# A four-value GpSimd operation behind the gathers of each tap of a deformable convolution

## The chip, the core and the metric

The kernel runs on one core of a Trainium2 chip. The core has five engines that run side by side, each with a queue of its own and in the order of that queue: TensorE (PE in the profile, its weight loads PEld) multiplies matrices, VectorE (DVE) and ScalarE (ACT) work elementwise, GpSimd (POOL) here issues indirect DMAs, and SyncE (SP) issues plain DMAs. Sixteen DMA engines, shared by all queues, move the data. The metric is the time of one execution on the device in microseconds (us), as the median of several runs.

## What is computed

The input is a picture batch of 4 x 256 channels x 64 x 64. Three deformable 3x3 convolutions follow a normalisation over the channels; then the result is added to the input and each of the 16,384 pixels goes as a token through a top-2-of-8 expert network. Of the reference, cut to the part that the change touches:

```python
K = 9
def _bilinear(feat, ys, xs):              # feat [B,C,H,W], ys and xs [B,K,H,W]
    y0, x0 = jnp.floor(ys), jnp.floor(xs)
    wy, wx = (ys - y0)[:, None], (xs - x0)[:, None]
    y0i, x0i = y0.astype(jnp.int32), x0.astype(jnp.int32)
    v00, v01 = _gather(feat, y0i, x0i), _gather(feat, y0i, x0i + 1)
    v10, v11 = _gather(feat, y0i + 1, x0i), _gather(feat, y0i + 1, x0i + 1)
    return v00*(1-wy)*(1-wx) + v01*(1-wy)*wx + v10*wy*(1-wx) + v11*wy*wx

def _deform_layer(x, w_off, b_off, w, b, dilation=1):
    om = conv3x3(x, w_off) + b_off        # 27 channels: 18 offsets, 9 masks
    ...
    sampled = _bilinear(x, ys, xs) * mask[:, None]
    return jnp.einsum('bikhw,oik->bohw', sampled, wk) + b[None, :, None, None]

for wo, bo, w, b in params:               # three layers
    x = jax.nn.relu(_deform_layer(x, wo, bo, w, b, dilation=1))
...
t = t + _L0_ffn_ref(_ln_t(t), ...)        # softmax gate, top 2 of 8 experts, gelu
```

For every pixel and every one of the nine taps, four neighbours are read at a place that the data decide, weighted, and multiplied by the tap's 256 x 256 weights.

## The kernel before

All arithmetic is in float32. There are twelve stages, one for each layer and picture; `run` (L1037) lists their order. A stage has eight blocks (NB) of 512 pixels, four tiles of 128 pixels each (TPB). `main_block` (L482) runs one block: nine taps (K), and for each tap two calls of `samples` (L494) with two tiles each. So a tap has four gathers, a block 36, and the whole program 12 x 8 x 36 = 3456, in 864 taps.

One gather (L503) is an indirect DMA on the POOL queue: for each of 128 pixels it fetches one row of 1024 floats, the four neighbours with 256 channels each, from a table in DRAM into a tile `g`. That is 512 KB. DVE then combines the neighbours in two steps (L509 into `g`, L514 into a tile `s`), ACT scales `s` (L517), TensorE transposes it (L532, in `turn`), ACT copies the transposed pairs to `sT` (L535), and `finish` multiplies them by the tap's weights into `acc` (L555). The pool of `g` tiles has GB = 10 buffers, two and a half taps: the eleventh gather waits until L514 has read the first. The pool of `s` tiles has eight. `turn` runs LAG = 2 pairs behind `samples`.

Work of other parts is woven in between the taps. `step` (L1001) advances the offset convolutions, the tables of the next layer and the gate; `pump` (L992) advances three lanes of the expert network. Of these, `fetch` (L790) puts three indirect DMAs on the POOL queue for each expert tile (weights `w` at L800, two token tiles `zt` at L812), and `combine_fetch` (L905) puts two (`gy`, L915) for each token tile. A helper `after` (L1007) pins an instruction behind a given one in the order that the framework works out; `self.gathered` is the newest gather, `self.last` the newest L514. So POOL's queue holds the gathers in order, and `w`, `zt` and `gy` between them behind the fourth gather of a tap. Apart from a few constants at the start, POOL has no arithmetic.

Of the kernel before, what the change touches and what calls it, by code (L numbers as in the profile page):

```python
# [8 lines left out]
F32 = mybir.dt.float32  # L9
I32 = mybir.dt.int32  # L10
AF = mybir.ActivationFunctionType
ALU = mybir.AluOpType
AX = mybir.AxisListType

P = 128
# [102 lines left out]
class Weave:  # L118
# [40 lines left out]
    def constants(self):  # L159
        nc, cst, ins = self.nc, self.cst, self.ins  # L160
        self.ident = cst.tile([P, P], F32, name="ident")
        make_identity(nc, self.ident)

        self.strips = cst.tile([P, Q], F32, name="strips")
        nc.vector.tensor_tensor(
            self.strips, self.ident[:, 0:Q], self.ident[:, Q : 2 * Q], ALU.add
        )
        for g in range(2, NQ):
            nc.vector.tensor_tensor(
                self.strips, self.strips, self.ident[:, g * Q : (g + 1) * Q], ALU.add  # L170
            )
        self.base = cst.tile([P, NB, TPB, K, 2], F32, name="base")
        nc.sync.dma_start(self.base.rearrange("p n t k d -> p (n t k d)"), ins["base"])
        self.wo, self.bo, self.bk = [], [], []
        for l in range(NL):
            queue = nc.sync if l == 0 else nc.gpsimd
            wo = cst.tile([P, K, CC, Q], F32, name=f"wo_{l}")
            queue.dma_start(wo, ins[f"conv_w_off{l}"].rearrange("k (c p) o -> p k c o", p=P))
            bo = cst.tile([P, 1], F32, name=f"bo_{l}")
            queue.dma_start(bo, ins[f"conv_b_off{l}"].rearrange("(o a) -> o a", a=1))  # L180
            bk = cst.tile([P, CC], F32, name=f"bk_{l}")
            queue.dma_start(bk, ins[f"conv_b{l}"].rearrange("(c p) -> p c", p=P))
            self.wo.append(wo)
            self.bo.append(bo)
            self.bk.append(bk)
        self.wk = [None] * K

    def room(self, tag, shape, name, gat=True):

        if not (self.starting and gat):  # L190
            return self.big.tile([P, *shape], F32, tag=tag, name=name)
        g = self.gat.tile([P, 2, 2, C], F32, tag="g", name=name)
        return g.rearrange("p x s f -> p (x s f)").rearrange("p (a b) -> p a b", a=shape[0])
# [288 lines left out]
    def main_block(self, i, n, wins):  # L482
        l, b = self.stages[i]
        plan = self.plans.pop((l, b, n))
        for k in range(K):
            for t0 in range(0, TPB, 2):
                ss = self.samples(i, n, k, t0, plan)
                self.pairs.append((i, n, k, t0, wins, ss))
                if len(self.pairs) > LAG:
                    self.turn()  # L490
            self.step(k)
            self.pump()

# [642 lines left out]
```

## Time and profile before

| | us |
|---|---|
| median of 10 runs | 6802.03 |
| lowest and highest | 6792.87, 6808.45 |
| the profiled execution's own time | 6816.85 |
| its span, first to last instruction | 6815.1 |

The profile is one execution. Its page gives the busy time of each engine, the same in 40 slices of 170 us, the chain of work that ended last, and the groups of instructions by source line. Further views of the same trace used below are tables of busy time by stretch (a busy time and, in brackets, a count for each engine, then the granted TensorE clock, the busy share of the DMA engines and GB/s), lists of waits (who waited for whom, us in total, times, the longest), and lines in order of time (start, duration, engine, line, operation, and in brackets the idle time before it and what ended it). A POOL duration of a DMA is the time in which GpSimd makes it, not the time in which the data move. The twelve stages start at 95, 614, 1054, 1502, 1961, 2459, 2977, 3508, 4055, 4569, 5083 and 5782 us of the span; the last gather is made at 6382, and behind it the last expert tiles are finished.

### The profile page before, as it was taken

The page shows a single profiled execution, that of the slowest core. Times are in us where ns is not written, and L with a number is a line of the kernel's source. Part 1 is how long each engine was busy: PE and PEld are TensorE (multiplying, and loading weights), DVE is VectorE, ACT ScalarE, POOL GpSimd, SP SyncE. Part 2 cuts the span into 40 slices and gives each one's busy share as a digit, 9 for nine tenths or more (in the row PEclk, how much of TensorE's full clock was granted, in tenths as well). Part 3 has the DMA queues.
Part 4 walks back from the last instruction along what each step waited for, and adds up shares of the span by engine and source line. Part 5 has one row for each costly group of instructions (what it writes and reads, how often), then busy time and mean ns, then how long its engine had stood idle before and what let it go on. Part 6 is the DMA issues. An engine that isn't in the chain of part 4 may idle for free.

```text
span 6815.1 us, 88985 instructions
## 1 busy us (share of the span) xinstructions
PE 6222.2 (91%) x26500; PEld 3526.9 (52%) x26500; DVE 4960.5 (73%) x11467; ACT 3280.5 (48%) x7141; POOL 4450.6 (65%) x4245
## 2 busy tenths in 40 slices
PE   7998888889999999999999999999998899988887
PEld 3443344444445555555555555555555566655665
DVE  6887778779999666668888777667878555688521
ACT  3554555555555445445554454445554444454322
POOL 4664766666667666666667777666666666677643
PEclk8999999999999999999999999999999999999998
DMA  8998999999999999899998999989998887899744
GB/s 283 355 352 301 365 350 374 356 350 389 379 394 353 326 353 335 323 332 354 352 360 310 361 360 369 325 328 341 346 344 301 294 291 272 290 350 331 243 136 125
DMA packets 800319, 2223.73 MB, mean 326 GB/s; under 512 B 104728, under 2 KB 302872, under 8 KB 794080
## 3 DMA queue, kind: packets, MB, share of 16 engines
q0 software_dynamic: 551200, 1947.35, 77.4%
q1 hardware_dynamic: 248640, 270.69, 11.7%
q8 instruction: 215, 3.52, 0.2%
q14 instruction: 264, 2.16, 0.1%
HBM read 2160.68 MB, written 196.40 MB: 346 GB/s over the span
## 4 chain that ended last, share of the span: by engine, by line
PE 71%; ACT 8%; DMA 7%; DVE 7%; issue 4%; POOL 3%; SPq 0%; ACTq 0%; DVEq 0%; POOLq 0%
PE acc L555 36%; PE tp L532 10%; PE ph L856 7%; PE po L357 7%; PE py L874 7%; DMA g<-tab,idx 5%; ACT sT L535 3%; DVE g L509 2%; ACT s L517 2%; DVE s L514 2%; POOL gy L915 1%; PE pm L371 1%; POOL g L503 1%; POOL zt L812 1%; PE tpv L325 1%
## 5 line engine op out<-in xcount | busy, mean ns | idle before, releaser
L503 POOL DMA_INDIRECT g<-tab,idx x3456 | 3652.7, 1057 | 1802.5 <-DVE s L514 659.4
L555 PE MATMUL acc<-sT,wk 128*128 128x512 f32 x6912 | 3389.3, 604 | 151.7 <-ACT sT L535 136.9
L509 DVE SCALAR_TENSOR_TENSOR g<-g,cf 128x512 f32<-128x512 f32 x3456 | 2559.0, 742 | 400.8 <-DMA g<-tab,idx 397.1
L514 DVE SCALAR_TENSOR_TENSOR s<-g,cf 128x256 f32<-128x256 f32 x3456 | 1660.4, 482 | 756.1 <-PE tp L532 474.1
L535 ACT COPY sT<-tp 128x512 f32<-128x512 f32 x1728 | 1001.3, 586 | 1836.7 <-PE tp L532 1831.9
L517 ACT ACTIVATE s<-s,cf 128x256 f32<-128x256 f32 x3456 | 1641.5, 508 | 447.1 <-DVE s L514 408.1
L555 PEld LDWEIGHTS acc<-sT,wk 128*128 128x128 f32 x6912 | 1162.6, 192 | 967.4 <-issue 655.9
L532 PEld LDWEIGHTS tp<-ident,s 128*128 128x128 f32 x6912 | 883.0, 143 | 1354.7 <-issue 654.8
L532 PE MATMUL tp<-ident,s 128*128 128x128 f32 x6912 | 1254.1, 281 | 190.9 <-ACT s L517 174.8
L856 PE MATMUL ph<-fzT,w 128*128 128x256 f32 x2608 | 687.6, 396 | 60.1 <-ACT fzT L844 33.6
L874 PE MATMUL py<-w,hT 128*128 128x256 f32 x2608 | 653.2, 389 | 31.8 <-ACT hT L866 26.7
L856 PEld LDWEIGHTS ph<-fzT,w 128*128 128x128 f32 x2608 | 483.9, 196 | 189.3 <-ACT fzT L844 61.5
L874 PEld LDWEIGHTS py<-w,hT 128*128 128x128 f32 x2608 | 475.3, 192 | 164.1 <-ACT hT L866 68.2
L866 ACT ACTIVATE hT<-ph,w 128x256 f32<-128x256 f32 x652 | 282.1, 471 | 450.3 <-PE ph L856 431.6
L812 POOL DMA_INDIRECT zt<-z,tok x326 | 334.6, 1026 | 161.7 <-issue 88.3
L357 PE MATMUL po<-win,wo 128*32 128x504 f32 (+1 forms) x2304 | 357.4, 598 | 5.0 <-ACT win L301 2.6
L800 POOL DMA_INDIRECT w<-in_W,wrow x163 | 178.1, 1092 | 266.4 <-issue 102.6
L915 POOL DMA_INDIRECT gy<-ys,slots x256 | 261.5, 1021 | 111.7 <-issue 65.2
L892 DVE TENSOR_TENSOR y<-py,w 128x512 f32<-128x512 f32 x163 | 111.5, 684 | 218.1 <-PE py L874 218.0
L930 DVE SCALAR_TENSOR_TENSOR ta<-gy,cw,ta 128x256 f32<-128x256 f32 x256 | 120.4, 480 | 137.3 <-DMA gy<-ys,slots 78.1
L357 PE MATMUL po<-win_pre,wo 128*32 128x504 f32 (+1 forms) x1152 | 187.0, 627 | 2.0 <-ACT om L366 2.0
L357 PEld LDWEIGHTS po<-win,wo 128*32 128x32 f32 x2304 | 73.1, 110 | 177.9 <-issue 142.7
(154 smaller groups left out, 2927.8 us busy)
## 6 DMA issues: line engine op xcount, KB each, us to landing
tab<-hv SPq DMA_DIRECT2D x512, 128.0 KB
g<-tab,idx POOLq DMA_INDIRECT x3456
ys<-y SPq DMA_DIRECT2D x163, 256.0 KB
tab<-h_pre SPq DMA_DIRECT2D x128, 256.0 KB
wk<-in_conv_w SPq DMA_DIRECT2D x99, 256.0 KB
xc_pre<-in_x SPq DMA_DIRECT2D x32, 512.0 KB
xr_tok<-in_x SPq DMA_DIRECT2D x32, 512.0 KB
t<-t_tok SPq DMA_DIRECT2D x32, 512.0 KB
```

Of the source, the lines that this page charges most:

```text
L357: nc.tensor.matmul(po[g * Q : (g + 1) * Q, :].rearrange("q (r w) -> q r w", w=W)[:, :, x0:x1], lhsT=self.wo[l][:, 3 * ky + kx, c, :], rhs= ...
L503: self.gathered = nc.gpsimd.indirect_dma_start(out=g.rearrange("p x s f -> p (x s f)"), out_offset=None, in_=self.table(*self.stages[i]), ...
L509: nc.vector.scalar_tensor_tensor(g[:, :, 0, :], g[:, :, 1, :], cf[:, j, 0:1], g[:, :, 0, :], ALU.mult, ALU.add,)
L514: self.last = nc.vector.scalar_tensor_tensor(s, g[:, 1, 0, :], cf[:, j, 1:2], g[:, 0, 0, :], ALU.mult, ALU.add)
L517: nc.scalar.activation(s, s, AF.Copy, scale=cf[:, j, 2:3])
L532: self.turned = nc.tensor.transpose(tp[:, c, u * P : (u + 1) * P], ss[u][:, c * P : (c + 1) * P], self.ident)
L535: nc.scalar.copy(self.sT[:, :, t0 * P : (t0 + 2) * P], tp)
L555: nc.tensor.matmul(acc[:, o, :], lhsT=self.wk[k][:, c, o * P : (o + 1) * P], rhs=sT[:, c, :], start=(k == 0 and c == 0), stop=(k == K - 1 ...
L812: self.nc.gpsimd.indirect_dma_start(out=zt, out_offset=None, in_=grp.zd, in_offset=bass.IndirectOffsetOnAxis(ap=grp.tok[:, j : j + 1], axi ...
L856: nc.tensor.matmul(ph[:, h, :], lhsT=w1[:, o : o + P], rhs=zT[:, c, :], start=(c == 0), stop=(c == CC - 1),)
L874: nc.tensor.matmul(py[:, u, :], lhsT=hT[h // 2][:, h % 2, u * P : (u + 1) * P], rhs=w2[:, h * C : (h + 1) * C], start=(h == 0), stop=(h == ...
L915: self.nc.gpsimd.indirect_dma_start(out=g, out_offset=None, in_=self.ys[grp.i % 3], in_offset=bass.IndirectOffsetOnAxis(ap=grp.slots[:, i, ...
```

## The change

A tile `rest` of 128 partitions x 4 floats is set to one at the start. Behind the four gathers of each tap, GpSimd raises it to the power of itself, in place; the value stays one and nothing reads it. `self.after(self.gathered)` pins the operation behind the tap's fourth gather.

```diff
@@ constants
         self.wk = [None] * K
+        self.rest = cst.tile([P, 4], F32, name="rest")
+        nc.gpsimd.memset(self.rest, 1.0)
@@ main_block
                 self.pairs.append((i, n, k, t0, wins, ss))
                 if len(self.pairs) > LAG:
                     self.turn()
+            with self.after(self.gathered):
+                self.nc.gpsimd.tensor_tensor(self.rest, self.rest, self.rest, ALU.pow)
             self.step(k)
             self.pump()
```

In the built program POOL's 4250 instructions keep their order, and 865 are added: the memset and 864 operations on `rest`, each ahead of the `w`, `zt` and `gy` fetches that stand behind the same gather. Each of the 864 waits for POOL's own semaphore, that is for the operation on `rest` of the tap before. The other engines issue the same instructions; their order differs in 102 of 17,802 places on PE, 56 of 11,469 on DVE, 58 of 7143 on ACT and 3 of 1166 on SP, where neighbours change places.

## The prediction

> **What bounds the kernel now.** First the page, for who is busy over the whole span and what a gather costs:
>
> ```profile
> span 6815.1 us, 88985 instructions
> PE 6222.2 (91%) x26500; PEld 3526.9 (52%) x26500; DVE 4960.5 (73%) x11467; ACT 3280.5 (48%) x7141; POOL 4450.6 (65%) x4245
> PEclk8999999999999999999999999999999999999998
> L503 POOL DMA_INDIRECT g<-tab,idx x3456 | 3652.7, 1057 | 1802.5 <-DVE s L514 659.4
> ```
>
> POOL seems to have a third of its time free. It has not: there is an idle stretch of about 0.30 us before each gather even where nothing is waited for, as the lines of POOL in order of time show, first from a stage without spare, then from one with it:
>
> ```profile
> 3812.93 0.94 POOL L503 DMA_INDIRECT g<-tab,idx  x1 [0.30 <-issue]
> 3814.18 0.95 POOL L503 DMA_INDIRECT g<-tab,idx  x1 [0.30 <-issue]
> 3817.94 1.19 POOL L800 DMA_INDIRECT w<-in_W,wrow  x1 [0.30 <-ACT s L517]
> 3819.44 1.02 POOL L812 DMA_INDIRECT zt<-z,tok  x1 [0.30 <-issue]
> ...
> 2511.58 0.97 POOL L503 DMA_INDIRECT g<-tab,idx  x1 [0.30 <-issue]
> 2512.86 0.94 POOL L503 DMA_INDIRECT g<-tab,idx  x1 [0.30 <-issue]
> 2519.37 1.21 POOL L503 DMA_INDIRECT g<-tab,idx  x1 [5.57 <-DVE s L514]
> ```
>
> So POOL is charged with its busy time and 0.305 us (the median idle time before an indirect DMA in the trace) for each instruction. Over the span: 4450.6 + 4201 x 0.305 = 5732 us of 6815, 84%. By stretch, from the table of busy times:
>
> ```profile
> 1502.00:1961.00 459.00, 418.38 (x1773) 218.04 (x1774) 421.99 (x1101) 246.01 (x543) 311.94 (x288) 0.97 1.01 387
> 2459.00:2977.00 518.00, 491.08 (x2092) 276.36 (x2091) 355.44 (x701) 257.72 (x575) 337.12 (x330) 1.00 0.91 333
> 3655.00:4121.00 466.00, 429.88 (x1853) 233.89 (x1852) 355.27 (x759) 225.84 (x495) 361.78 (x343) 0.99 0.97 355
> 6018.00:6212.00 194.00, 161.28 (x608) 87.04 (x608) 175.04 (x460) 90.87 (x188) 152.12 (x137) 0.95 0.97 359
> ```
>
> The last bracketed pair of a row is POOL's. Stage 3 (1502 to 1961): 311.9 + 288 x 0.305 = 400 of 459, 59 us spare on 72 taps, 0.8 us a tap; there DVE (92%) and the DMA engines bound. Stage 5 (2459 to 2977): 438 of 518, 80 us spare, 1.1 us a tap; TensorE bounds at 95%. But 3655 to 4121, where `w`, `zt` and `gy` fetches stand between the gathers: 361.8 + 343 x 0.305 = 466.4 of 466. POOL is full. So it is from 6018 to 6212: 193.9 of 194. These are 63 and 27 taps. The waits of DVE say what that means for the rest of the core; the first row is from 3655 to 4121, the second from 2459 to 2977:
>
> ```profile
> DVE g L509 <- DMA g<-tab,idx: 76.4, 66, 6.0
> ...
> DVE g L509 <- DMA g<-tab,idx: 2.8, 5, 0.8
> ```
>
> In stage 5 DVE hardly ever waits for a gather. From the semaphore updates of the landings, gathers there lie ready for a median of 7.7 us before L509 takes them; from 3855 to 4055 it is 0.03 to 0.13 us. So a later gather is covered in most stages and is late at once where POOL is full.
>
> **The change part by part.** Removed: nothing. Moved: two neighbours change places in under 1% of the positions on PE, DVE, ACT and SP; no row of these is longer for it, and I cost it at 0, hidden by the same cover of several us; without that cover a swap is worth at most one L509, 0.74 us, some fifty times, 37 us either way. The memset stands among the table fills before 95 us, where POOL then idles 57 us for the first table: 0. The wait for POOL's own semaphore is for the operation of the tap before, over 5 us old: 0. No DMA and no other queue gets an instruction.
>
> Added: 864 operations on four values. Queued behind each on POOL are the next gather, or `w`, `zt` and `gy`; DVE waits for the gathers, TensorE for `zt` and `w`. The trace has no power and no arithmetic between gathers, so its price X is bounded. Below by POOL's small operations at the start:
>
> ```profile
> 37.35 0.31 POOL L247 TENSOR_SCALAR_AFFINE_SELECT upper<-ones 128x128 f32<-128x128 f32 x1
> 37.60 0.15 POOL L259 IOTA part_i<- 128x1 int32 x1
> 37.69 0.26 POOL L264 IOTA row_i<- 128x128 int32 x1
> ```
>
> IOTA on one value takes 0.15 us and starts before its neighbour has ended, the next one 0.09 us later. Above by the longest thing that POOL does again and again, a gather, 1.06 us. A power is nearer to the arithmetic rows than to a gather, but above the simplest: I take X = 0.4, about the geometric mean of 0.15 and 1.06. To this comes the idle time: one more of 0.305 at most; at least none, and if the 0.30 us runs on while the operation is at work, up to 0.305 of X is hidden. I take 0.1. So the delay d for each tap is 0.5 us, with 0 (0.15 hidden in the gap) and 1.36 (1.06 + 0.305) as ends.
>
> Then I walked the POOL rows of the trace in order: d is added behind every fourth gather; each idle time is used up for what it has over 0.305; a lag that exceeds the time for which that gather would lie ready is added to the end and shifts all that follows. That charges DVE's lateness in full. Result, in us added to the end, by stage 0 to 11, for d = 0.5: 2, 6, 2, 2, 9, 3, 0, 29, 10, 4, 18, 30, sum 115. The check by hand: the two full stretches are 90 taps x 0.5 = 45 us; the remaining 70 come from shorter full stretches in stages 4 and 8 to 11, and from each stage's first gathers. For other delays: d = 0.1 gives 20, 0.2 gives 42, 0.4 gives 90, 0.7 gives 170, 1.0 gives 305, 1.36 gives 548. Above 0.7 it bends upwards because it passes the spare of 0.8 to 1.1 us of the other stages.
>
> The profiled execution's own time is 6816.85, 1.75 over its span and 0.2% over the median of 6802.03. The walk is a difference, so it goes on the median: 6802 + 115 = 6917.
>
> [...]
>
> **Rivals.**
> (A) The operation is as long as a gather. d is 1.0 to 1.36, POOL has no spare in nearly any stage and becomes the bound of the whole: 7107 to 7350. For it: no row shows a power, and AFFINE_SELECT and IOTA do far simpler things. Against: four values for each partition, next to 128 in 0.31 us.
> (B) It is hidden. It fits into the 0.30 us that POOL idles before each gather, d below 0.07: 0 to 14 us, 6802 to 6816. For it: the overlapping starts above. Against: the 0.30 is there after every gather, even when the wait was long over, so it looks like work done in sequence.
> (C) Faster, by pacing. A gather takes 0.94 us at the least and 1.057 on average; the stretch of 0.117 us may come from four gathers being made in a row beside DVE's two-input L509. If the pause takes it off the next gather and is itself hidden as in B, d is -0.117 and at the walk's 205 us for each us the time is 6802 - 24 = 6778; off all four, 0.47 us a tap, 6706. It decides once the operation costs less than it gives, under about 0.12 us beyond the gap. Against: in the full stretch above 0.94 and 0.95 appear in a row without any pause, so neighbours are not what stretches a gather.
>
> **How the numbers follow.** The forecast (d from 0.07 to 1.0, own range 6816 to 7107) has 0.60, A 0.15, B 0.10, C 0.15. The time is 6917. The range of 6780 to 7230 takes in the forecast, B, the small end of C and half of A; about 0.08 is left out on either side. What a measurement can tell from no change is about 0.2%, 14 us: faster is C, 0.15; same is B, 0.10; slower is the forecast and A, 0.75.
>
> **What would show it.** In the changed profile: the operation's own duration near 0.4 us and the idle before the next gather 0.3 to 0.4; POOL's busy time up by about 350 us; POOL's waits for L514 down; L509's waits for gathers longer, above all from 3655 on and in the last two stages, with stages 1, 2, 3 and 6 as long as before to within some us. The forecast is wrong if the stages without expert work grow as much as the full ones (A), if gathers behind the operation start as soon as before (B), or if the mean gather falls clearly under 1.057 us (C).

## The result, and the profile after

| | before | after |
|---|---|---|
| median | 6802.98 us (28 runs) | 7026.14 us (8 runs) |
| lowest and highest | 6792.87, 6815.32 | 7014.40, 7041.40 |
| ratio, with its 95% interval | | 1.0328 [1.0319, 1.0337] |
| profiled execution, span | 6816.85, 6815.1 | 7031.39, 7029.6 |

Slower by 223 us in the medians and by 214.5 us in the spans. The page of the changed kernel, the rows that answer to those of before (line numbers are four higher from the tap's gather on: L503 is now L507, L509 is L513, L514 is L518, L532 is L536):

```profile
span 7029.6 us, 89847 instructions
PE 6310.5 (90%) x26500; PEld 3557.4 (51%) x26500; DVE 5081.9 (72%) x11467; ACT 3331.1 (47%) x7141; POOL 5490.9 (78%) x5110
...
PEclk9999999999999999999999999999999999999998
...
L507 POOL DMA_INDIRECT g<-tab,idx x3456 | 3655.2, 1058 | 1072.7 <-issue 536.5
```

POOL's busy time rose by 1040 us, not by the 350 that four tenths of a us each would give, while a gather still takes 1058 ns (1057 before). The groups by line put the whole rise on the new operation, in two views (all of it; then shortest, median and longest in ns):

```profile
L494 POOL TENSOR_TENSOR rest<-rest 128x4 f32<-128x4 f32 x864 | 1018.6, 1179 | 19.2
```
```profile
L494 POOL TENSOR_TENSOR rest<-rest x864: 1034/1062/3869, 91.6 to 6601.2; 128x4 f32<-128x4 f32 x173
```

POOL in order of time, at one tap in stage 5 (start, duration, and in brackets the idle time before):

```profile
2629.78 0.94 POOL L507 DMA_INDIRECT g<-tab,idx  x1 [0.30 <-issue]
2631.02 0.95 POOL L507 DMA_INDIRECT g<-tab,idx  x1 [0.31 <-issue]
2631.97 1.06 POOL L494 TENSOR_TENSOR rest<-rest 128x4 f32<-128x4 f32 x1
2633.22 0.99 POOL L507 DMA_INDIRECT g<-tab,idx  x1 [0.19 <-issue]
2634.52 0.95 POOL L507 DMA_INDIRECT g<-tab,idx  x1 [0.30 <-DVE g L513]
```

The operation starts as the fourth gather ends, lasts as long as a gather, and the idle stretch behind it is 0.19 in place of 0.305 us. So a tap of POOL's costs d = 1.179 (mean) + 0.026 (idle before, median) + 0.188 (idle behind, median) - 0.305 (the idle that stood there anyway) = 1.09 us more. The forecast had 0.5.

Stage 3, stage 5 and the two stretches in which POOL was full, found again by the same blocks of the program:

```profile
1552.00:2041.00 489.00, 425.04 (x1779) 223.42 (x1778) 429.87 (x1118) 252.57 (x543) 408.38 (x361) 0.94 0.97 361
2560.00:3080.00 520.00, 491.34 (x2068) 275.83 (x2066) 373.15 (x704) 255.68 (x570) 424.91 (x403) 0.99 0.93 333
```
```profile
3753.00:4286.00 533.00, 467.39 (x1899) 247.20 (x1899) 365.45 (x767) 242.05 (x510) 433.83 (x410) 0.95 0.90 315
6202.00:6417.00 215.00, 168.44 (x602) 87.48 (x601) 176.42 (x456) 92.85 (x186) 177.77 (x159) 0.92 0.89 313
```

Charge POOL, the last bracketed pair, as before, but with 0.21 us of idle time for each operation on `rest` and 0.305 for each DMA that does not stand behind one. Stage 3, with 72 operations among 361 instructions: 408.4 + 72 x 0.21 + 217 x 0.305 = 490 of 489 us. Stage 5: 424.9 + 15 + 259 x 0.305 = 519 of 520. From 3753: 433.8 + 64 x 0.21 + 282 x 0.305 = 533 of 533. From 6202: 177.8 + 27 x 0.21 + 105 x 0.305 = 215 of 215. POOL is now full in all four, and was so in only two. Stage 3 grew by 28 us and stage 5 by 2, because stage 5 had 80 us to spare and stage 3 only 59.

The waits of DVE (total us, times, longest), before and then after:

```profile
DVE s L514 <- PE tp L532: 474.1, 553, 4.7
DVE g L509 <- DMA g<-tab,idx: 397.1, 250, 10.7
```
```profile
DVE g L513 <- DMA g<-tab,idx: 1068.8, 1097, 10.1
...
DVE s L518 <- PE tp L536: 13.9, 23, 1.9
```

DVE's wait for gathers grew by 672 us, and its wait for TensorE (the second combining step, which needs a free `s` tile) fell by 460. So as much as two thirds of the new lateness came out of a wait that DVE had anyway. That the difference, 212 us, meets the growth of the span to 3 us is partly chance: DVE's busy time grew by 121 us besides, and its other waits and gaps shrank by 119. POOL's own wait for a free `g` tile, 659 us before (the row of L503 in the prediction), is almost gone, as it must be when POOL is the one that lags:

```profile
POOL g L507 <- DVE s L518: 29.7, 73, 5.1
```

The growth by stage (from the last L514 or L518 of a stage to that of the next; row 3 is the walk of the prediction run again at the measured d of 1.09; us):

| stage | 0 | 1 | 2 | 3 | 4 | 5 | 6 | 7 | 8 | 9 | 10 | 11 | tail | sum |
|---|---|---|---|---|---|---|---|---|---|---|---|---|---|---|
| measured | -5 | 23 | 27 | 28 | 24 | 2 | 4 | 52 | 11 | 9 | 5 | 39 | -4 | 214.5 |
| walk, d = 0.5 | 2 | 6 | 2 | 2 | 9 | 3 | 0 | 29 | 10 | 4 | 18 | 30 | | 115 |
| walk, d = 1.09 | 10 | 32 | 25 | 22 | 27 | 11 | 8 | 63 | 25 | 20 | 45 | 68 | | 357 |
| 72 x 1.09 less POOL's spare | 0 | 0 | 21 | 20 | 19 | 0 | 3 | 53 | 14 | 9 | 0 | 24 | | 163 |

The last row is a plain ledger: 78 us of added work in a stage, less the idle time over 0.31 us that POOL had there in the trace of before (79, 92, 57, 58, 59, 80, 75, 25, 64, 69, 111, 54 us), never below nothing. It is nearest to what was measured. Where it misses most, in stage 1, 44 of the 92 us of spare lay in the first block, where most of them could not be used: the other seven blocks have 63 x 1.09 - 48 = 21 us, against 23 measured. With these it makes 184 of the 214.5 us; the other 30, half of them in stage 11, it does not explain.

### The profile page after: what moved, and what is told of

It reads as the page before. It is cut to its first block, busy times and chain, and to the rows that moved or that the text cites. A ratio compares the mean times of both kernels' runs of the same rounds, so it can differ in the third digit from the quotient of the medians.

```text
span 7029.6 us, 89847 instructions
## 1 busy us (share of the span) xinstructions
PE 6310.5 (90%) x26500; PEld 3557.4 (51%) x26500; DVE 5081.9 (72%) x11467; ACT 3331.1 (47%) x7141; POOL 5490.9 (78%) x5110
## 5 line engine op out<-in xcount | busy, mean ns | idle before, releaser
L507 POOL DMA_INDIRECT g<-tab,idx x3456 | 3655.2, 1058 | 1072.7 <-issue 536.5
L513 DVE SCALAR_TENSOR_TENSOR g<-g,cf 128x512 f32<-128x512 f32 x3456 | 2570.0, 745 | 1085.7 <-DMA g<-tab,idx 1068.8
L521 ACT ACTIVATE s<-s,cf 128x256 f32<-128x256 f32 x3456 | 1677.2, 508 | 927.6 <-DVE s L518 856.5
L518 DVE SCALAR_TENSOR_TENSOR s<-g,cf 128x256 f32<-128x256 f32 x3456 | 1685.4, 490 | 335.0 <-PE tp L536 13.9
L536 PEld LDWEIGHTS tp<-ident,s 128*128 128x128 f32 x6912 | 884.2, 145 | 1495.7 <-ACT s L521 808.4
L536 PE MATMUL tp<-ident,s 128*128 128x128 f32 x6912 | 1279.6, 285 | 288.7 <-ACT s L521 265.9
L494 POOL TENSOR_TENSOR rest<-rest 128x4 f32<-128x4 f32 x864 | 1018.6, 1179 | 19.2
L919 POOL DMA_INDIRECT gy<-ys,slots x256 | 268.2, 1047 | 102.0 <-issue 62.5
```

The costliest lines, as they stand in the source:

```text
L494: self.nc.gpsimd.tensor_tensor(self.rest, self.rest, self.rest, ALU.pow)
L507: self.gathered = nc.gpsimd.indirect_dma_start(out=g.rearrange("p x s f -> p (x s f)"), out_offset=None, in_=self.table(*self.stages[i]), ...
L513: nc.vector.scalar_tensor_tensor(g[:, :, 0, :], g[:, :, 1, :], cf[:, j, 0:1], g[:, :, 0, :], ALU.mult, ALU.add,)
L518: self.last = nc.vector.scalar_tensor_tensor(s, g[:, 1, 0, :], cf[:, j, 1:2], g[:, 0, 0, :], ALU.mult, ALU.add)
L521: nc.scalar.activation(s, s, AF.Copy, scale=cf[:, j, 2:3])
L536: self.turned = nc.tensor.transpose(tp[:, c, u * P : (u + 1) * P], ss[u][:, c * P : (c + 1) * P], self.ident)
```

## The experiments

All are edits of the changed kernel unless said. Theory T is: POOL's added time per tap, d, decides, and is added to the end where POOL has no spare left. The kernel before took 6804 us in the first set of four.

**The price or the switch?** A multiplication in place of the power:

```diff
-self.nc.gpsimd.tensor_tensor(self.rest, self.rest, self.rest, ALU.pow)
+self.nc.gpsimd.tensor_tensor(self.rest, self.rest, self.rest, ALU.mult)
```

> A multiplication of the same four values in place of the power, in the same place. Theory (the loss is the time that POOL spends on the power, where it has no spare): a simple operation takes 0.1 to 0.2 us, and with 0.02 us idle before and 0.19 behind it, in place of one idle time of 0.30, the delay is 0.01 to 0.1 us a tap: 0 to 20 us on the end, ratio to before 1.000 to 1.003. Rival (each switch from gathers to arithmetic and back costs, whatever the operation, as when code is loaded anew): the operation takes about as long as the power, 1.0 us or more, and the ratio is about 1.033.

Measured: 6820.81 us, ratio 1.0023 [1.0014, 1.0032].

```profile
L494 POOL TENSOR_TENSOR rest<-rest x864: 205/298/2963, 95.3 to 6391.6; 128x4 f32<-128x4 f32 x173
```

The same 864 turns from gathers to arithmetic and back cost 17 us in all. So it is not the turn from one to the other, but what the power computes: 1034 ns at the shortest in place of 205. The multiplication was longer than expected all the same, and its loss stayed within the expected 20 us. With the mean of 385 ns and 0.15 us of idle behind, d is 0.25; the walk gives 54 us for it, three times too much.

Nor is it that GpSimd's arithmetic slows VectorE: L514 takes 482 ns on average before, 490 with the power and 493 with the multiplication, which costs almost nothing.

**Less of the same.** `rest` as one value for each partition, in place of four:

```diff
-self.rest = cst.tile([P, 4], F32, name="rest")
+self.rest = cst.tile([P, 1], F32, name="rest")
```

> The power on one value for each partition in place of four. If the time is by value, 1.06 us falls to about 0.3 to 0.4 us, the delay to 0.2 to 0.3 us a tap, and the end is 30 to 60 us later, ratio 1.004 to 1.009. If the time is by instruction, it stays near 1.06 us and the ratio near 1.033.

Measured: 6845.81 us, 1.0062 [1.0049, 1.0075].

```profile
L494 POOL TENSOR_TENSOR rest<-rest x864: 571/676/3315, 96.5 to 6424.5; 128x1 f32<-128x1 f32 x173
```

The operation fell between the two cases that were expected, 0.3 to 0.4 us and 1.06: a part of its price is by value and a part by instruction. d is 0.749 (mean) + 0.02 + 0.173 - 0.305 = 0.64, less than the spare of 0.8 us a tap in the open stages. The span grew by 38 us, 29 of them in stage 7 and 17 in stage 11 (the rest of the stages gave back 8): only where POOL was full, as T has it. The walk gives 150 us for this d, three and a half times as much as was measured.

**Where the price is paid.** The operation only behind the 90 taps of the ten blocks without spare, and then only behind the other 774:

```diff
+full = (i, n) in ((7, 2), (7, 3), (7, 4), (7, 5), (7, 6), (7, 7), (8, 0), (11, 3), (11, 4), (11, 5))
+if full:          # the second kernel: if not full
     with self.after(self.gathered):
         self.nc.gpsimd.tensor_tensor(self.rest, self.rest, self.rest, ALU.pow)
```

> The power stands only behind the 90 taps of the ten blocks in which POOL had no spare before (blocks 2 to 7 of stage 7, block 0 of stage 8, blocks 3 to 5 of stage 11). Theory: there each delay of some 1.1 us goes to the end, as these blocks grew by 84 us in the changed kernel: 75 to 100 us, ratio 1.011 to 1.015. Rival (the operation costs the same wherever it stands, through DVE, the DMA engines or the clock): 90 of 864 taps, 223 x 90 / 864 = 23 us, ratio 1.003.

> The power stands behind the other 774 taps only. Theory: what is left of 223 us when the ten full blocks' 84 us are taken away, 120 to 145 us, ratio 1.018 to 1.021. Rival (same cost everywhere): 223 x 774 / 864 = 200 us, ratio 1.029.

Measured: 6883.92 us, 1.0113 [1.0098, 1.0127] for the 90, and 6939.56 us, 1.0193 [1.018, 1.0206] for the 774.

```profile
L496 POOL TENSOR_TENSOR rest<-rest x90: 1034/1112/1833, 3655.7 to 6286.8; 128x4 f32<-128x4 f32 x90
```

80 us for 90 operations is 0.89 us each; 136 us for 774 is 0.18 each. A cost that is the same wherever the operation stands would have put 23 us on the first and 200 on the second, so it is ruled out. The two together, 216 us, are nearly the 223 of the whole change. In the seven full blocks of stages 7 and 8 the growth was 64 us on 63 taps, 1.02 a tap: there nearly all of d reaches the end.

**What was left to ask.** The next set of four: whether the growth follows d over the spare of 0.8, whether another buffer helps, and whether spreading the token fetches helps the kernel before.

```diff
-self.rest = cst.tile([P, 4], F32, name="rest")
+self.rest = cst.tile([P, 2], F32, name="rest")      # and [P, 8] in the second kernel
```

> The power on two values. From one value (shortest 0.57 us) and four (1.03 us) the operation is 0.42 us and 0.154 us a value, so 0.73 us at the shortest, about 0.87 on average, and with 0.02 us before and 0.18 behind it in place of 0.305 the delay is about 0.77 us a tap. That is below POOL's spare in every stage outside the full blocks (0.8 us a tap and more). Theory with a threshold at the spare: the ten full blocks give 50 to 65 us, the rest at most 30: 50 to 90 us, ratio 1.008 to 1.013. Rival (the walk of the prediction, which charges every lateness of a gather): about 200 us, ratio 1.029.

> The power on eight values: 1.65 us at the shortest, about 1.8 on average, a delay of about 1.7 us a tap, above the spare of every stage. Theory (72 taps times the delay less the stage's spare, and the full blocks in full): 550 to 700 us, ratio 1.08 to 1.10; from four values to eight the time grows by about 0.6 us for each tap, nearly the operation's own growth. Rival (cost by number of operations, not by length): ratio 1.03 to 1.04.

```diff
-GB = 10
+GB = 11
```

> The changed kernel with eleven buffers for gathers in place of ten. Theory (POOL has no time left, its throughput sets the pace): the buffer gives nothing, ratio to before 1.030 to 1.034. Rival (the gathers come late because they are not issued far enough ahead): a tenth more run-ahead takes part of the loss back, ratio below 1.027.

```diff
@@ the kernel before, end of an expert group
-put(1, lambda m=m: self.combine_fetch(grp, m + ahead))
+put(1 if grp.last else 3, lambda m=m: self.combine_fetch(grp, m + ahead))
```

> The kernel before, without the power, with the gy gathers of the first four expert groups spread over four taps each in place of two. The order of the work is changed, nothing of it left out. Theory (a full POOL costs time before the change as well): the full blocks of stage 7 shrink by 10 to 50 us in sum and others take a little of it back, ratio 0.993 to 1.000. Rival (TensorE or DVE bounds there too, or a longer tail of the sums collides with the next group): 1.000 or above.

Measured, beside a kernel before that itself took 7621.11 us here (7588 to 7654, 17 runs) where it had taken 6804: two values 7186.33, 0.9432 [0.9397, 0.9466]; eight values 7466.68, 0.9782 [0.9746, 0.9819]; eleven buffers 7115.94, 0.934 [0.9312, 0.9369]; the spread fetches 7659.25, 1.0054 [1.0031, 1.0076]. The sign of the whole change is turned round, and what was expected of two and of eight values, as ratios to 6804, can't be tried against such a set. What can be used is the price of the operation, from the shortest of each:

```profile
L494 POOL TENSOR_TENSOR rest<-rest x864: 714/796/2969, 90.9 to 6721.5; 128x2 f32<-128x2 f32 x173
```
```profile
L494 POOL TENSOR_TENSOR rest<-rest x864: 1664/1681/2637, 95.6 to 7032.5; 128x8 f32<-128x8 f32 x173
```

571, 714, 1034 and 1664 ns for 1, 2, 4 and 8 values: some 0.41 us and 0.156 more for each value. Spreading the fetches gains nothing here; whether it would where the kernel before takes 6803 us, and POOL bounds a part of it, was not tried. Whether the eleventh buffer gains is not decided: the changed kernel was not in this set, and took 7069 in another. So the rival that gathers are only issued too late, and not made too slowly, was not tested in the first surrounding; against it stands that POOL's charge fills the stretches above (490 of 489 us in stage 3).

**Is it the set or the kernel?** Two values and eight again, in a further set:

> The power on two values once more, as the last four kernels ran on a chip where the kernel before takes 7621 us and not 6803, and where TensorE's signals came late (over 2 us behind the last matmul 262 times in the kernel without a power, 85 times with it on four values; twice in every run before). If this chip is like the first one (before at about 6803 us): ratio 1.008 to 1.013 by the threshold theory, 1.029 by the walk. If it is like the second: 0.94 to 0.95, which would say that the gain there is repeatable and that chip and kernel must be told apart.

> The power on eight values once more, for the same reason. On a chip with before at about 6803 us: a delay of about 1.7 us a tap, over every stage's spare, 550 to 700 us, ratio 1.08 to 1.10. On a chip with before at about 7620 us: 0.975 to 0.985; the longer pause leaves fewer late signals of TensorE (34 against 155 with two values) but POOL's own time takes the gain back.

Measured: the kernel before 7516.99 us; two values 7069.35, 0.9423 [0.9399, 0.9447]; eight 7460.2, 0.993 [0.991, 0.9949]. So the gain with two values comes back as expected; with eight values less is left of it than the 0.975 to 0.985 expected. Last, the changed kernel itself, and a pause that lies on DVE and takes nothing of POOL:

```diff
-with self.after(self.gathered):
-    self.nc.gpsimd.tensor_tensor(self.rest, self.rest, self.rest, ALU.pow)
+with self.after(self.last):        # rest is 128 x 1024, set by DVE
+    self.nc.vector.tensor_tensor(self.rest, self.rest, self.rest, ALU.mult)
```

> The changed kernel itself once more. On a chip where the kernel before takes about 6803 us: ratio 1.030 to 1.036. On one where it takes about 7500 to 7620 us: 0.93 to 0.945, from the 0.934 of the version with eleven buffers, with 60 to 120 late signals of TensorE.

> The pause on another engine: behind the last L514 of each tap DVE multiplies a tile of 128 x 1024 values by itself (about 1.2 us, as L599 took for its addition of that size), POOL gets nothing. On a chip with before at about 6803 us: DVE has about 140 us spare in most stages, less in stages 0 and 3, for 72 x 1.2 = 86 us; 30 to 150 us, ratio 1.004 to 1.022. On a chip with before at about 7500 to 7620 us it tells what the pause does there: if any pause that slows the pace helps TensorE, the ratio is 0.93 to 0.98 and the late signals fall under 150; if it must be a pause of POOL and its gathers, the ratio is 1.00 or above and the late signals stay near 262.

Measured: the kernel before 7499.6 us; the changed kernel 7069.13, 0.9426 [0.9413, 0.9439]; the pause on DVE (1218 ns at the median) 7456.54, 0.9945 [0.9931, 0.9959]. The changed kernel takes almost what it took at first (7026), the kernel before 700 us more than it took at first. The ratio of the changed kernel is as expected, its late signals (42, counted below) are fewer than the 60 to 120 expected. The pause on DVE met neither of its two cases: the late signals fell below 150, to 107, but the ratio stayed above 0.98. So it is not that the operation had become cheaper; the kernel before had become slow.

The traces show at what. The chains that ended last, of the spread kernel (which is the kernel before but for some fetches) and of the changed kernel in these later sets, shares of the span:

```profile
PE 67%; ACT 10%; issue 8%; another core or an unknown queue 7%; DVE 4%; DMA 3%; POOL 1%; ACTq 0%; SPq 0%; DVEq 0%; POOLq 0%
```
```profile
PE 55%; DMA 14%; DVE 9%; issue 9%; POOL 7%; ACT 6%; another core or an unknown queue 0%; SPq 0%; DVEq 0%; POOLq 0%; ACTq 0%
```

"Another core or an unknown queue" is a wait whose releaser the profile can't name; 7% of 7636 us is some 530 us. The chain of the kernel before in the first surroundings has no such share. There is no other core here. One such wait of the spread kernel in order of time, first TensorE, then ScalarE:

```profile
664.29 4.45 PE L357 MATMUL po<-win_pre,wo 128*32 128x512 f32 x36
680.48 1.91 PE L371 MATMUL pm<-strips,om 128*128 128x27 f32 x8 [11.74 <-ACT om L366]
```
```profile
669.11 0.51 ACT L517 ACTIVATE s<-s,cf 128x256 f32<-128x256 f32 x1 [4.35 <-DVE s L514]
679.74 0.69 ACT L366 ACTIVATE om<-po,bo 128x512 f32<-128x512 f32 x1 [10.12 <-remote]
```

The 36 matmuls into `po` end at 668.7; TensorE's semaphore is counted up only at 679.65, and ScalarE, which reads `po`, starts at 679.74. For 11 us TensorE waits for ScalarE and ScalarE for a signal of work that is done. Such signals, over 2 us after the end of the last matmul before them, number: 2 (9 us in sum) in the kernel before, the changed kernel and the first set; 262 (1071 us) in the spread kernel; 155 (521) and 78 (254) with two values; 85 (262) with eleven buffers; 42 (139) in the changed kernel again; 34 (104) and 23 (71) with eight values; 107 (425) with the pause on DVE. Signals of VectorE and ScalarE are late no more than twice in any of them. (The later traces lack 18 to 25% of TensorE's semaphore records, those of the first sets 0.1% at most, so the counts are low bounds if anything.) The longer GpSimd pauses between taps, the fewer they are, in each set. From the eleven buffers with four values to eight values in the second set the time rises by 351 us while the late signals fall by 158: together 509 us on 864 taps, 0.59 a tap, and the operation grew by 0.60. That is an estimate, for it counts a us of lateness as a us of time, and in the spread kernel 1071 us of lateness stand beside a span only 821 us longer than that of the kernel before. It agrees with theory T's cost going on in these sets while something else is given back, but does not show it.

What makes the signals late was not found. The records give chip number 5 for the first set of four and 15, 6 and again 5 for the later ones; the last set came 42 minutes after the first. So the chip's number alone does not tell the two surroundings apart. Whether the late signals and the lost records have one cause, the recording itself included, was not tried. Also, the kernel before itself was not profiled in them, only the spread kernel, which is next to it. What a pause on DVE costs without late signals was not measured either.

## Why the prediction was right, and where it was not

The direction and the range held: 7026 lies between 6780 and 7230, 109 us over the forecast. That the point is not further off is luck: two errors point in opposite directions. The mechanism with the 0.60 did not hold as it was put, for the measured d of 1.09 lies outside the forecast's own 0.07 to 1.0 and inside rival A's 1.0 to 1.36.

**The price X.** Taken as 0.4 us, measured 1.18 on average; with the idle time d is 1.09 in place of 0.5. The upper bound of 1.06 from the gather row was closer to it than the geometric mean of the two bounds, and the shortest power (1.034) all but is that bound. The rows that X was leaned on, IOTA and AFFINE_SELECT (0.15 to 0.31 us), are of the size of the multiplication (0.205 us); the power is five times that. The idle time was taken as +0.1: measured 0.026 + 0.188 - 0.305 = -0.09. So a part of a gap is saved, as the alternative that was named there allows. But the idle behind the operation does not shrink as the operation grows (0.15 us behind the multiplication, 0.18 behind eight values), so it is not shown that the gap runs on while the operation is at work.

**The walk.** "That charges DVE's lateness in full" is the step that failed. At the true d it gives 357 us against 214.5, at 0.64 150 against 38, at 0.25 54 against 9 in the profile and 17 in the medians. It treats a late gather as a late end. But DVE, once late, hardly waits for a free `s` tile any more: 460 us of that wait went away, and what a late gather takes from it need not reach the end. Had this cover been seen, with d at 0.5 the sum would have been near the 45 us of the full stretches, 6847; one value, with d = 0.64, came to 6846.

**What was read rightly.** POOL's charge of busy time and 0.305 us for each DMA: by it POOL was full in 3655 to 4121 and 6018 to 6212, and there 84 us came on 90 taps (61.8 and 22.6 by the ends of the blocks), 0.94 a tap. Also that a stage pays for what exceeds its spare: of stages 1, 2, 3 and 6, forecast to stay as long as before, 6 did (4 us on 75 us of spare), while 1, 2 and 3 grew by 23 to 28, since d passed their 0.8 us.

**The rivals.** A had the operation right, as long as a gather with d between 1.0 and 1.36, and POOL as the bound far beyond its two full stretches, as stages 3 and 5 above show; but not of every stage, for 0, 5, 6 and 10 hardly grew. Its 7107 at the least came from the walk and was too much by 81 us; the forecast's own range, up to 7107, held for the same reason. What happened is A's mechanism at a lower price. B fell with the first run: the operation is three times the gap, and even the multiplication cost 17 us. C fell too: the mean gather stayed at 1058 ns. With the multiplication it fell to 1047, some 0.04 us a tap, too little for C. That the change made the kernel faster in the later sets is hardly C's mechanism either: there the mean gather is 1052 ns in the changed kernel and 1067 in the spread one, 0.06 us a tap or some 50 us in all, against a gain of 430 that goes with fewer late signals of TensorE.

**What was taken at nothing.** Places changed on other engines, the memset and the semaphore wait: the multiplication has them all, and with its own d they come to 17 us together.

One number needs a word on the clock. TensorE's mean granted clock fell from 0.977 to 0.967. The records hold two clocks, full and half, and the time at half rose from 309 to 468 us; the shortest such stretch was 3.41 us, and the others are whole multiples of it but for one that the end cuts off. In the trace of before, 51 windows of 3.41 us at full clock were followed by half clock; by the matmul rows TensorE was idle 1.9 us of such a window at the median, and all of it in 3. In the 1851 windows that were followed by full clock it was idle for 1.9 us at most. The time at half was longer where the span was: 320 us of 6824 with the multiplication, 364 of 6891 with the 90 operations alone, 367 of 6919 with the 774 alone. How much of the 214.5 us is the slower clock and how much the waits themselves was not separated.

## What to carry to other kernels

Price an operation by what it computes as well as by its size: when no row shows it, the bound on the far side deserves as much weight as the near one. When work is added to a queue that feeds the bound, first take the spare of each stage, in the queue's full charge and not in its busy time, and compare it with the added time for each unit; then, before a late input is charged to the end, look for the waits that the consumer has for others, for here it was these that shrank. And a few per cent found in one place are a statement on that place: run both kernels again elsewhere before the change is taken or thrown away.

## What the runs showed of the hardware that was not expected

A power on GpSimd took 0.571, 0.714, 1.034 and 1.664 us at the shortest for 1, 2, 4 and 8 values for each of 128 partitions, a multiplication of four 0.205; beside the gathers the means were 0.12 to 0.18 us higher. At the median GpSimd idled 0.305 us between two indirect DMAs, 0.026 between a gather and the power of four values behind it, and 0.15 to 0.19 between the arithmetic and the next DMA, whether the arithmetic took 0.2 us or 1.7.

The kernel before took 6803 us in two sets and 7500 to 7621 in three others, the changed kernel 7026 in one and 7069 in another. In the traces from the later sets TensorE's completion signals came more than 2 us late up to 262 times, and with powers on GpSimd between the taps 23 to 155 times. The change is thus a loss of 3.3% in the one surrounding and a gain of 5.7% in the other, whose traces show late signals; why they are late stays open. In the first set no kernel was faster than the one before; in the later ones the changed kernel and the one with two values, both 7069, had the shortest times, and eleven buffers, 0.934, the lowest ratio to the kernel before beside them.
